# A Macaron block on one core: the experts' first layer as seven block products for four, its operand sums on GpSimd and VectorE, and the slot search of two experts at once

## The chip, the core and the metric

The kernel runs on one core of one Trainium2 chip. The metric is device time in microseconds of one execution. Before the change the median of 9 runs is 836.21 us (830.43 to 840.21). One execution was also taken with the hardware profiler; its own time is 834.38 us.

The engines are named as the profile does: PE is the matrix engine (TensorE), PEld its weight load, DVE the vector engine, ACT the scalar engine, POOL GpSimd, SP the engine that only issues DMAs. L364 is line 364 of the kernel before.

## What is computed

8 x 1024 rows of 256 float32 values go through three residual steps: half a mixture of experts, an attention-like layer with a fast-weight memory, and half the same mixture of experts again. The change concerns the mixture of experts alone:

```python
E, F, CAP = 8, 1024, 320
logits = tokens @ gate_w
probs = softmax(logits)
expert_idx = argmax(probs)
mask1 = one_hot(expert_idx, E)
pos = cumsum(mask1, axis=0) - 1
sec_mask = mask1[:, :, None] * one_hot(pos, CAP)
combine_weights = probs[:, :, None] * sec_mask
expert_input = einsum('tec,td->ecd', sec_mask, tokens)
h = relu(einsum('ecd,edf->ecf', expert_input, w1))
expert_output = einsum('ecf,efd->ecd', h, w2)
out = einsum('tec,ecd->td', combine_weights, expert_output)
```

Each token goes to one expert, and each expert takes its first 320 tokens. `tokens` are layer-normed rows. For each expert `h` is a product of 320 x 256 by 256 x 1024 with a relu (the first layer), and the output is `h` by 1024 x 256 (the second layer). Everything is float32.

## The kernel before

`macaron` (L1276) runs `experts` (the first stage), `attention`, and `experts` again (the second stage). In the profiled execution the first layers of the first stage begin at 53.89 us and those of the second at 661.40 us. The attention between them is not edited. Inside all three the order of the program is the order of the work: `tc.manual_schedule` keeps each engine's instructions as the Python calls emit them, and the waits between engines follow from the tiles that are written and read.

**Finding the slots.** `Slots` (L149) works out which rows each expert gets. `begin(q)` (L197) does the part that two experts share: two matmuls into `d_ps`, an ACT copy into `dg` (L206), a matmul `b_ps` (L209), and a DVE comparison into `began` (L212). `tokens(e)` (L215) then does, for one expert, three matmuls into `r_ps` (L222). They use 64 of PE's 128 rows, the upper or lower half by the expert's parity. Six DVE instructions (L235 to L243; ten for expert 0) make the row numbers `get` and `put` from them. `exps` and `gates` (L174, L178) make the gate values, and `spread` (L187) writes them to DRAM (`gate_d`).

**Rows in and out.** `gather(e)` (L276) fetches an expert's 320 rows by three indirect DMAs that POOL issues (two of 128 rows, one of 64 that is held in a different form), and `gate_of(e)` (L287) its gate values by three more. `center` (L295) subtracts the mean of each row on DVE: `bn_stats`, `bn_aggr` and a subtraction for each of the three row tiles. `turn` (L305) transposes the rows on PE, six transposes into two banks, and two ACT copies (L318) bring them to `xT`, the first layer's moving operand, 2 x 128 partitions by 320 columns. The results go out by indirect DMAs from POOL, one for the 64-row part (L400) and one for each of two tiles of 128 rows (L421).

**Startup of a stage** (L326 to L338). On PE: `begin(0)`, the counts of experts 0 and 1, `begin(1)`, 13 idle matmuls (`keep(13)`, L85, which write to a bank that nobody reads and keep PE running while rows arrive), and the turn of expert 0 with two idle matmuls in it. DVE does tokens 0 and 1, `began` for the next two experts, and centers the rows as they come.

**One expert** (the loop at L351 to L428). POOL first gets the gathers and gates of expert e+2, SP the weights of e+1 (`Weights.load`, L254 and L256, 1 MB each, two buffers), and DVE centers the rows of e+1. Then PE does:
- the first layer, 8 blocks of 128 outputs, each two matmuls of 128x128 weights by 320 columns into one bank (L364), followed by ACT's relu out of the bank (L371);
- the turn of expert e+1;
- the second layer of the 64-row part, 16 matmuls of 128 columns over the two halves of PE's columns (L387), with DVE's scaling and residual into `xh` (L397) and a scatter;
- the second layer of the two full tiles, 8 matmuls of 256 columns each (L411), with DVE (L418) and a scatter after each.

The dictionary `searches` (L340) puts the other searches between the first layer's blocks: the spread and tokens 2 and 3 and `begin(2)` in expert 0, tokens 4 and 5 and `begin(3)` in expert 1, tokens 6 and 7 in expert 2. The PSUM banks are three each with the tags `h` (first layer, `r_ps`, `b_ps`) and `t` (turns, spread), and two with the tag `y` (second layer, idle, `d_ps`).

Of the kernel before, what the change touches and what calls it, by code (L numbers as in the profile page):

```python
# [18 lines left out]
P = 128  # L19
# [3 lines left out]
D = 64  # L23
# [125 lines left out]
class Slots:  # L149
# [10 lines left out]
    def __init__(self, sh, pool, pp, dr, routed):  # L160
        self.sh, self.pool, self.pp, self.dr, self.routed = sh, pool, pp, dr, routed
# [15 lines left out]

    def gates(self):  # L178

        nc, routed = self.sh.nc, self.routed  # L180
        tot = self.pool.tile([P, 2, NI], F32, name="tot")
        nc.vector.tensor_reduce(tot[:, 0], routed.dl.rearrange("p e i -> p i e"), AX.X, ALU.add)
        nc.vector.reciprocal(tot[:, 0], tot[:, 0])
        nc.vector.tensor_tensor(routed.by_tile(tot[:, 1]), tot[:, 0], routed.r16, ALU.mult)
        self.by_row = tot[:, 1]

    def spread(self, _):  # L187

        nc = self.sh.nc
        t_ps = self.pp.tile([P, 512], F32, tag="t", name="t_ps")  # L190
# [6 lines left out]
    def begin(self, q, between=lambda n: None):  # L197

        nc, sh, pool, pp = self.sh.nc, self.sh, self.pool, self.pp

        d_ps = pp.tile([P, 512], F32, tag="y", name="d_ps", bufs=2)
# [6 lines left out]
        b_ps = pp.tile([P, 512], F32, tag="h", name="b_ps")  # L208
# [5 lines left out]

    def tokens(self, e):  # L215

        nc, sh, pool, pp = self.sh.nc, self.sh, self.pool, self.pp
        part = slice(e % 2 * D, (e % 2 + 1) * D)
        r_ps = pp.tile([P, 512], F32, tag="h", name="r_ps")
        rv = r_ps[:, : NS * (P + 1)].rearrange("p (s r) -> p s r", s=NS)  # L220
        for s in range(NS):
            nc.tensor.matmul(  # L222
                rv[:, s, :],
                lhsT=self.began[part, s * P : (s + 1) * P],
                rhs=self.dg[part, e // 2, :],
                start=True,
                stop=True,
            )
# [4 lines left out]
        for a, b in ((0, 1), (1, NS)) if e == 0 else ((0, NS),):  # L233
# [4 lines left out]
            nc.vector.tensor_reduce(t, upto[:, a:b], AX.X, ALU.add)  # L238
            nc.vector.scalar_tensor_tensor(t, t, float(-P), rv[:, a:b, P], ALU.add, ALU.add)
# [6 lines left out]
class Weights:  # L246


    def __init__(self, nc, pool, w1, w2):
        self.nc, self.pool, self.w1, self.w2, self.at = nc, pool, w1, w2, {}  # L250
# [7 lines left out]


def experts(sh, routed, src, dst, weights, dr, name, idle=0):  # L260
# [3 lines left out]

    nc, tc = sh.nc, sh.tc
    with ExitStack() as st:
        rp = st.enter_context(tc.tile_pool(name=f"{name}_r", bufs=1))
        ep = st.enter_context(tc.tile_pool(name=f"{name}_e", bufs=2))
        pp = st.enter_context(tc.tile_pool(name=f"{name}_p", bufs=3, space=PSUM))
# [1077 lines left out]
```

## Time and profile before

| | |
|---|---|
| median of 9 runs | 836.21 us (830.43 to 840.21) |
| the profiled execution | 834.38 us |
| its span, first to last instruction | 832.5 us |
| mean granted PE clock | 0.951 of full speed |
| first layers of stage 1 / stage 2 begin | 53.89 / 661.40 us |
| DVE, ACT, POOL busy | 55%, 42%, 57% of the span |

The page of a profile gives the share of the span for which each engine was busy, then the span in 40 slices (each digit is a busy share in tenths; for the line PEclk it is the clock that PE was granted, 9 is full). The views of the trace used below are the timeline of one engine (start, length, engine, line, operation, output<-inputs, shapes, count, and in brackets how long the engine had been idle and what ended that), the groups (all instructions of one line and shape: busy time and mean duration in ns, then the idle time before them), and windows (busy times of the engines in a stretch). A float32 matmul is two records. "x32" over 8.78 us is thus 16 matmuls. Ends of matmuls are modelled and overlap the next start, so the time that a matmul takes from the engine is read from start to start.

### The profile page before, as it was taken

The numbers are of one execution on the slowest core, as the hardware profiler recorded it, in microseconds if no ns is written. First come the engines' busy times: TensorE is split into PE (matmuls) and PEld (weight loads), VectorE is DVE, ScalarE is ACT, GpSimd is POOL, SyncE is SP. The second block draws the span as 40 slices with busy tenths as digits, with TensorE's granted clock in tenths as the row PEclk, the third lists the DMA queues.
The fourth block names the chain that finished last, engine by engine and source line by source line (L and its number), as shares of the span: only waits on it lengthen the run. The fifth ranks groups of instructions, "written<-read, shape, count | busy, mean of one in ns | idle before, by whom it ended". The sixth has DMA issues, their size and how long they took to land. (4 is left out here: it accounts for less than half of the span.)

```text
span 832.5 us, 13850 instructions
## 1 busy us (share of the span) xinstructions
PE 763.3 (92%) x5304; PEld 554.7 (67%) x5304; DVE 454.5 (55%) x939; ACT 346.6 (42%) x738; POOL 471.3 (57%) x610
## 2 busy tenths in 40 slices
PE   7996899999848999899999999999978988999997
PEld 5665677887625576666757576676764666778875
DVE  7770332222236988888887868978744613322220
ACT  5411212222136585767666755766332212122221
POOL 6525344441123688888888868886754353444411
PEclk9997899999958999999999979999799989999999
DMA  9993345442034233354454523334325623454420
GB/s 299 370 379 115 103 137 184 139 142 67 27 97 103 77 78 103 83 176 100 152 130 135 138 78 110 79 127 103 128 74 179 243 74 93 133 179 139 143 72 19
DMA packets 110946, 110.41 MB, mean 133 GB/s; under 512 B 12384, under 2 KB 103904, under 8 KB 110880
## 3 DMA queue, kind: packets, MB, share of 16 engines
q1 hardware_dynamic: 73312, 66.50, 26.7%
q10 hardware_dynamic: 31680, 31.46, 12.1%
q0 software_dynamic: 5888, 11.57, 4.1%
q8 instruction: 42, 0.69, 0.3%
q14 instruction: 24, 0.20, 0.1%
HBM read 78.80 MB, written 30.64 MB: 131 GB/s over the span
## 5 line engine op out<-in xcount | busy, mean ns | idle before, releaser
L371 ACT ACTIVATE hT<-ph 128x320 f32<-128x320 f32 x128 | 55.6, 437 | 236.1 <-PE ph L364 209.3
L364 PE MATMUL ph<-xT,w1t 128*128 128x320 f32 x512 | 148.0, 442 | 0.9 <-ACT xT L318 0.9
L411 PE MATMUL py<-w2t,hT 128*128 128x256 f32 x512 | 120.4, 394 | 7.2 <-issue 7.2
L364 PEld LDWEIGHTS ph<-xT,w1t 128*128 128x128 f32 x512 | 97.0, 192 | 39.8 <-issue 2.0
L411 PEld LDWEIGHTS py<-w2t,hT 128*128 128x128 f32 x512 | 99.5, 197 | 24.5 <-issue 10.8
L397 DVE SCALAR_TENSOR_TENSOR xh<-py,gate,xg 64x128 f32<-64x128 f32 x32 | 11.2, 350 | 130.8 <-PE py L387 105.9
L418 DVE SCALAR_TENSOR_TENSOR xo<-py,gate,xg 128x256 f32<-128x256 f32 x32 | 15.5, 484 | 95.1 <-PE py L411 91.5
L287 POOL DMA_INDIRECT gate<-gate_d,get x48 | 45.6, 949 | 36.2 <-DMA gate_d<-gates 22.2
L1111 PE MATMUL pre<-wg,xT 128*128 128x256 f32 x256 | 61.7, 402 | 2.6 <-DVE m L870 2.6
L775 PE MATMUL pre<-xT,w 128*64 128x512 f32 x256 | 61.4, 603 | 0.5 <-ACT kk L807 0.5
L1111 PEld LDWEIGHTS pre<-wg,xT 128*128 128x128 f32 x256 | 50.8, 202 | 11.5 <-DVE m L870 3.2
L1155 POOL TENSOR_TENSOR xo<-xo,xr 128x512 f32<-128x512 f32 x32 | 42.9, 1353 | 21.0 <-DVE xo L1149 16.9
L678 ACT ACTIVATE xt<-xt,ln_nm,lx_t 128x256 f32<-128x256 f32 x64 | 34.4, 592 | 24.5 <-POOL ln_nm L673 24.5
L1149 DVE SCALAR_TENSOR_TENSOR xo<-tail,rs,gate 128x256 f32<-128x256 f32 x64 | 27.1, 477 | 25.5 <-DMA out<-xo 15.7
L964 DVE TENSOR_TENSOR gc<-ehd,c 128x1536 f32<-128x1536 f32 x16 | 40.0, 2539 | 0.3
L421 POOL DMA_INDIRECT out<-xo,put x16 | 15.8, 990 | 39.5 <-DVE xo L418 37.3
L421 POOL DMA_INDIRECT x<-xo,put x16 | 15.8, 988 | 39.3 <-DVE xo L418 37.2
L775 PEld LDWEIGHTS pre<-xT,w 128*64 128x64 f32 x256 | 15.8, 136 | 30.4 <-issue 22.4
L876 POOL TENSOR_TENSOR abq<-qq,ab 128x512 f32<-128x512 f32 x16 | 34.5, 2156 | 2.3 <-DMA ab<-kept 2.2
L387 PE MATMUL py<-w2t,hT 128*64 128x128 f32 x512 | 32.7, 276 | 2.5 <-issue 2.5
L400 POOL DMA_INDIRECT out<-xh,put x8 | 8.1, 1008 | 46.9 <-DVE xh L397 46.9
L685 PE MATMUL pre<-ident,xt 128*128 128x128 f32 x128 | 21.0, 298 | 14.7 <-ACT xt L678 13.3
(256 smaller groups left out, 1642.3 us busy)
## 6 DMA issues: line engine op xcount, KB each, us to landing
w1t<-w_in SPq DMA_DIRECT2D x16, 1024.0 KB
w2t<-w_in SPq DMA_DIRECT2D x16, 1024.0 KB
xt<-hidden_in SPq DMA_DIRECT2D x16, 512.0 KB
x<-xt SPq DMA_DIRECT2D x16, 512.0 KB
xt<-x ACTq DMA_DIRECT2D x16, 512.0 KB
xr<-x ACTq DMA_DIRECT2D x16, 512.0 KB
x<-xo ACTq DMA_DIRECT2D x14, 512.0 KB
out<-xo ACTq DMA_DIRECT2D x14, 512.0 KB
```

The source lines that it names most:

```text
L287: nc.gpsimd.indirect_dma_start(out=gate[:, s : s + 1], out_offset=None, in_=slots.gate, in_offset=bass.IndirectOffsetOnAxis(ap=slots.get[: ...
L364: nc.tensor.matmul(ph[:, :CAP], lhsT=a[:, c, f * P : (f + 1) * P], rhs=at[:, c, :], start=(c == 0), stop=(c == 1),)
L371: nc.scalar.activation(hT[:, f, :], ph[:, :CAP], AF.Relu)
L387: nc.tensor.matmul(py[h * D : (h + 1) * D, :P], lhsT=hT[:, f, 2 * P :], rhs=b[:, f, h * P : (h + 1) * P], start=(f == 0), stop=(f == FC - ...
L411: nc.tensor.matmul(py[:, :H], lhsT=hT[:, f, s * P : (s + 1) * P], rhs=b[:, f, :], start=(f == 0), stop=(f == FC - 1),)
L421: nc.gpsimd.indirect_dma_start(out=dst, out_offset=bass.IndirectOffsetOnAxis(ap=slots.put[:, e, s : s + 1], axis=0), in_=xo[:, s, :], in_o ...
L678: self.nc.scalar.activation(x, x, AF.Identity, bias=u.nm[:, j : j + 1], scale=u.r16[:, j : j + 1])
L775: self.nc.tensor.matmul(ps[self.half[r], :], lhsT=self.w3[:, k, f * D : (f + 1) * D], rhs=u.xT[:, k].rearrange("h (p r t) -> h p r t", p=N ...
L876: self.nc.gpsimd.tensor_tensor(u.abq[:, n], u.kv[2], u.ab[:, n], ALU.mult)
L964: self.nc.vector.tensor_tensor(u.gc[:, layer], g.unsqueeze(2).to_broadcast([P, B, 3, D]), u.c3.rearrange("s n j -> s j n").unsqueeze(3).to ...
L1111: self.nc.tensor.matmul(ps[:, q * H : (q + 1) * H], lhsT=u.xT[:, k, j * P : (j + 1) * P], rhs=self.wg[:, k, :], start=(k == 0), stop=(k == 1),
L1155: self.nc.gpsimd.tensor_tensor(u.xo[h][:, two], u.xo[h][:, two], u.xr[h][:, two], ALU.add)
```

## The change

**First layer.** A product of a 2 x 2 block matrix by a 2 x 2 block matrix takes eight block products; with sums of blocks beforehand and afterwards it takes seven (Strassen's method in Winograd's form). Here the blocks of the weights are 128 x 128 (two halves of the 256 inputs, two neighbouring blocks of 128 outputs), and those of the rows are 128 x 160 (the 320 columns in halves, `HC = 160`). For each pair g of output blocks (four pairs for an expert) there are seven matmuls of 160 columns in place of four of 320, so 28 for an expert in place of 16.

The sums of the weights are four `tensor_tensor` of 128 x 512 on GpSimd for each expert, the first two after the first layer of the expert before, the others after its 64-row scatter. They go to a tile `s` of two buffers. The sums of the rows, `row_sums`, are three DVE instructions per expert. The sums of the products are spread over DVE and ACT: each pair of output blocks has an ACT copy (`p6`), four DVE additions (`u`, `v`, one of 320 columns into `hT`, one of 160), and three relus of which two read and write SBUF. The signs are turned so that the centered rows and the relus carry a scale of -1.

```diff
+    def sums(self, e, some):
+        (a11, a12), (a21, a22) = self.parts(e)
+        if e not in self.s:
+            self.s[e] = self.pool.tile([P, 4, FC // 2, P], F32, tag="s", name="s")
+        s = self.s[e]
+        for n in some:
+            x, y, op = (
+                (a21, a22, ALU.add),
+                (s[:, 0], a11, ALU.subtract),
+                (a11, a21, ALU.subtract),
+                (a12, s[:, 1], ALU.subtract),
+            )[n]
+            self.nc.gpsimd.tensor_tensor(s[:, n], x, y, op)
...
+        def row_sums(xT):
+            t = ep.tile([P, 4, HC], F32, tag="xs", name="xs")
+            v = xT.rearrange("p c (j n) -> p (c j) n", j=2)
+            nc.vector.tensor_tensor(t[:, 0:2], v[:, 1:4:2], v[:, 0:2], ALU.subtract)
+            nc.vector.tensor_tensor(t[:, 2], v[:, 3], t[:, 0], ALU.subtract)
+            nc.vector.tensor_tensor(t[:, 3], v[:, 2], t[:, 2], ALU.subtract)
+            return t
...
+            def one(self, g):
+                x = self.x[g] = bank("x", "x")
+                self.product(x[:, :HC], self.s[:, 1], g, self.t[:, 2])
+                self.product(x[:, HC : 2 * HC], self.a[0][0], g, self.b[:, 0, 0], stop=False)
+                u = self.u[g] = ep.tile([P, HC], F32, tag="u", name="u", bufs=3)
+                p6 = ep.tile([P, HC], F32, tag="p6", name="p6")
+                nc.scalar.copy(p6, x[:, :HC])
+                nc.vector.tensor_tensor(u, x[:, HC : 2 * HC], p6, ALU.add)
+            def two(self, g):
+                z = self.z[g] = bank("z", "z")
+                self.product(z[:, :HC], self.s[:, 2], g, self.t[:, 1])
+                self.product(z[:, HC : 2 * HC], self.a[1][1], g, self.t[:, 3])
+                self.product(z[:, 2 * HC : 3 * HC], self.s[:, 0], g, self.t[:, 0], stop=False)
+                v = ep.tile([P, 1, HC], F32, tag="v", name="v")
+                nc.vector.tensor_tensor(v[:, 0], z[:, :HC], self.u[g], ALU.add)
+                nc.vector.tensor_tensor(
+                    self.hT[:, 2 * g + 1, :].rearrange("p (j n) -> p j n", j=2),
+                    z[:, HC : 3 * HC].rearrange("p (j n) -> p j n", j=2),
+                    v.to_broadcast([P, 2, HC]),
+                    ALU.add,
+                )
+            def three(self, g):
+                x = self.x[g]
+                self.product(x[:, HC : 2 * HC], self.a[0][1], g, self.b[:, 1, 0], start=False)
+                nc.scalar.activation(self.hT[:, 2 * g, :HC], x[:, HC : 2 * HC], AF.Relu, scale=-1.0)
+            def four(self, g):
+                z = self.z[g]
+                self.product(z[:, 2 * HC : 3 * HC], self.s[:, 3], g, self.b[:, 1, 1], start=False)
+                nc.vector.tensor_tensor(self.hT[:, 2 * g, HC:], z[:, 2 * HC : 3 * HC], self.u[g], ALU.add)
+            def relu(self, f, a=0):
+                h = self.hT[:, f, a:]
+                nc.scalar.activation(h, h, AF.Relu, scale=-1.0)
...
+            for g in range(G):
+                first.one(g)
+                if g > 0:
+                    first.three(g - 1)
+                first.two(g)
+                if g > 0:
+                    first.four(g - 1)
+                    first.relu(2 * g - 1)
+                    first.relu(2 * g - 2, HC)
             if e + 1 < E:
-                xT = turn(xn)
+                xT = ep.tile([P, 2, CAP], F32, tag="xT", name="xT")
+                turn(xn[e + 1], 0, xT)
+            first.three(G - 1)
+            first.relu(2 * G - 1)
+            if e + 1 < E:
+                turn(xn[e + 1], 1, xT)
+            first.four(G - 1)
+            first.relu(2 * G - 2, HC)
+            if e + 1 < E:
+                weights.sums(e + 1, (0, 1))
+                t = row_sums(xT)
```

The PSUM banks are now two each for `t`, `x`, `z` and `y`. The 64-row part takes its blocks in the order 0 to 5, 7, 6. `center` keeps `bn_stats` and `bn_aggr` on DVE and has ACT form mean minus row; it works on expert e+2 and stands after the first full tile of the second layer. The gates of an expert are fetched one expert ahead, not two.

**Searches.** `tokens` is split. `counts(q)` does the matmuls of two experts in turns, one on each half of PE's rows, into two banks; `in_two(e)` does an expert's DVE part from them.

```diff
+        for s in range(NS):
+            for r in range(2):
+                part = slice(r * D, (r + 1) * D)
+                nc.tensor.matmul(
+                    self.count[r][:, s, :],
+                    lhsT=self.began[part, s * P : (s + 1) * P],
+                    rhs=self.dg[part, q, :],
+                    start=True,
+                    stop=True,
+                )
```

The searches that remain in the loop stand after the 64-row part (`search(e, 0)` and `search(e, 1)`): `begin(2)` in expert 0, the counts and tokens of 4 and 5 in expert 1, `begin(3)` in expert 2, the counts and tokens of 6 and 7 in expert 3. Those of experts 2 and 3 move to the startup:

```diff
         keep(idle)
-        slots.begin(0, keep)
-        rows, gates = [], []
+        slots.begin(0, "y", keep)
+        slots.exps()
+        slots.counts(0)
+        rows, gates, xn = [], [], {}
         for e in range(2):
             slots.tokens(e)
             rows.append(gather(e))
-        slots.begin(1)
-        slots.exps()
+        weights.sums(0, range(4))
+        slots.begin(1, "y")
+        slots.totals()
+        slots.counts(1)
+        slots.tokens(2)
         keep(13)
-        xT = turn(center(rows[0]), keep)
+        third = slots.in_two(3)
+        xn[0] = center(rows[0], (0,))
         slots.gates()
+        center(rows[0], (1,), xn[0])
+        next(third)
+        center(rows[0], (2,), xn[0])
+        next(third, None)
+        rows.append(gather(2))
+        xT = ep.tile([P, 2, CAP], F32, tag="xT", name="xT")
+        for c in range(2):
+            turn(xn[0], c, xT, keep)
+        t = row_sums(xT)
+        slots.spread()
+        xn[1] = center(rows[1])
+        gates = [gate_of(0), gate_of(1)]
```

In the startup the turn of expert 0 is two turns of three transposes, each with two idle matmuls in it, so four in all.

## The prediction

> **What bounds the kernel now.** I read the page's busy shares and its 40 slices first. In them PE's weight-load line is called PEld.
>
> ```profile
> PE 763.3 (92%) x5304; PEld 554.7 (67%) x5304; DVE 454.5 (55%) x939; ACT 346.6 (42%) x738; POOL 471.3 (57%) x610
> ...
> PE   7996899999848999899999999999978988999997
> ...
> PEclk9997899999958999999999979999799989999999
> ```
>
> PE is busy for 92% of the span, and every other engine for under 60%. So a stage costs what PE takes for it, plus the waits that reach PE. The attention between the two expert stages is not edited, and I leave its time as it is. The clock line has dips (the 7 and the 5, the two 7s later); those in the expert stages come back below.
>
> Then PE's timeline, where a row is start, length, engine, line, and in brackets the idle time before it. Expert 6 of the second stage is an undisturbed expert:
>
> ```profile
> 790.64 8.78 PE L364 MATMUL ph<-xT,w1t 128*128 128x320 f32 x32
> 799.25 0.86 PE L312 MATMUL pt<-ident,xn 128*128 128x128 f32 x6
> 800.04 1.97 PE L387 MATMUL py<-w2t,hT 128*64 128x128 f32 x32
> 801.94 7.17 PE L411 MATMUL py<-w2t,hT 128*128 128x256 f32 x32
> ```
>
> No brackets: PE never waits. The next expert's L364 starts at 808.95. From start to start the expert takes 18.31 us: first layer 8.61, turn 0.79, 64-row part 1.90, two token tiles 7.01. A float32 matmul is two records, so 16 matmuls are 32 records and one record of 320 columns is 8.61 / 32 = 269 ns. In the second layer one of 256 columns is 7.01 / 32 = 219 ns, of 128 columns (the turns and the two-half pairs aside) about 109.
>
> The windows by expert show that the first experts of a stage are not like that (columns: length; busy time of PE, PEld, DVE, ACT, POOL; granted clock; DMA):
>
> ```profile
> 53.89:85.59 31.70, 24.62 (x121) 18.58 (x122) 8.42 (x27) 4.95 (x13) 13.42 (x14) 0.84 0.54 178
> 85.59:111.92 26.33, 23.07 (x121) 17.48 (x120) 8.56 (x27) 4.30 (x11) 8.73 (x9) 0.94 0.39 122
> ```
>
> Expert 0 of the first stage takes 31.7 us. Expert 2 takes 20.44. The searches of expert 0 account for 3.2 (two trains of 0.86, one `begin` of 1.2, a spread of 0.27); 31.7 - 18.31 - 3.2 = 10.2 are lost. By the same sum the lost time is 5.1 and 0.4 in experts 1 and 2, and 7.2, 3.9 and 0.4 in the second stage (28.72, 25.13 and 20.44 us there): 27 us in all. The largest piece, on PE and on DVE:
>
> ```profile
> 79.27 6.49 PE L411 MATMUL py<-w2t,hT 128*128 128x256 f32 x16 [6.73 <-issue]
> ```
> ```profile
> 78.50 0.71 DVE L397 SCALAR_TENSOR_TENSOR xh<-py,gate,xg 64x128 f32<-64x128 f32 x2 [14.01 <-remote]
> ```
>
> PE stands 6.73 us for nothing that the profile shows, and then runs the second tile in 6.32 us instead of 3.50, at half clock. I can't say what releases it, and this is the main doubt of the sum.
>
> **Part 1, the first layer.** Before: 16 matmuls of 320 columns, 8.61 us. After: per pair of blocks 7 products of 160 columns, 28 per expert. The trace has no 160-column matmul. Between 109 ns (128 columns) and 219 (256) a line gives 0.86 ns a column, so 136 ns a record, 0.272 a product, 28 x 0.272 = 7.62: **-0.99 us** an expert, if PE never waits.
>
> It will wait. The sums after the products are a chain: `two(g)` needs the z bank that `four(g-2)`'s DVE addition left, and the loop has two z banks. From that addition's end to the next one of the same parity: PE hears it (0.055, the latency seen between DVE and PE) and runs up to the third product (about 1.02 with its drain), DVE does v (0.32) and hT (0.49), PE's `four` lies under these, DVE adds (0.32): 2.16 us for each g with the gaps. PE's own work for a g is 7 x 0.272 = 1.90. The stall is 0.26 at g = 2 and 3, **+0.52**. The DVE durations are estimates between rows of the trace with one PSUM operand: 128 wide 0.29, 256 wide 0.42, 384 wide 0.55. At 0.40 and 0.60 nothing is gained, at 0.30 and 0.47 there is 0.6. I take -0.47 for the 14 experts with a successor (the split turn covers the loop's tail) and +0.1 for the two last: **-6.4 us**, bounds 0 and -13.9.
>
> **Part 2, the searches.** Before, six trains of 0.87 us stand in each stage's stream (L222, six records each). After, the counts of two experts go over alternate halves of the rows. The startup shows the price, because two trains are adjacent there:
>
> ```profile
> 647.81 1.26 PE L222 MATMUL r_ps<-dg,began 64*128 64x129 f32 x12
> 649.00 0.49 PE L203 MATMUL d_ps<-tri,mask_b 128*128 128x128 f32 x2
> ```
>
> 12 records in 1.19 us. Two such pairs remain in the stream (the third moves to the startup): 5.2 - 2.4 = 2.8 a stage, **-5.6 us**. At no gain from alternating it is 1.7 a stage; no less.
>
> **Part 3, the startup.** In before the 13 idle matmuls ran while DVE worked through the first searches:
>
> ```profile
> 650.07 0.38 PE L209 MATMUL b_ps<-dg,before 128*128 128x1 f32 x2 [0.36 <-ACT dg L206]
> 650.31 8.63 PE L85 MATMUL idle<-jrow,ident 128*128 128x384 f32 x26
> 658.78 0.38 PE L312 MATMUL pt<-ident,xn 128*128 128x128 f32 x2
> ...
> 661.40 0.81 PE L364 MATMUL ph<-xT,w1t 128*128 128x320 f32 x2 [0.45 <-ACT xT L318]
> ```
>
> After, `counts(1)` stands ahead of them in PE's order and needs `began(1)`, which DVE ends at 46.02 (653.87 in the second stage). So: 46.05 + 1.3 of counts = 47.35; 8.46 of idle matmuls = 55.8; two turns in sequence with four idle matmuls, 0.80 + 4 x 0.65 + 0.45 of copy = 3.85; row_sums 0.47 + 0.31 + gaps = 0.9; first product at 60.6, against 53.89. That is +6.7, and by the same sum +7.0 in the second stage: **+13.7 us**. What DVE does here besides (token 2, the split centre) ends under the idle matmuls; it is worth up to 3 us a stage if it doesn't.
>
> **Part 4, GpSimd.** Four 128x512 additions per expert join POOL's queue. Before, an expert has nine indirect DMAs at 1.25 to 1.29 us from start to start:
>
> ```profile
> 717.51 0.99 POOL L276 DMA_INDIRECT xg<-x,get  x1 [0.30 <-issue]
> 718.80 0.97 POOL L276 DMA_INDIRECT xg<-x,get  x1 [0.30 <-issue]
> ```
>
> That is 7.6 for gathers and gates and 3.8 for scatters, the third of which waits about 1.3 more for the landing of the second. Now the rows for the additions:
>
> ```profile
> L1155 POOL TENSOR_TENSOR xo<-xo,xr 128x512 f32<-128x512 f32 x32 | 42.9, 1353 | 21.0 <-DVE xo L1149 16.9
> L876 POOL TENSOR_TENSOR abq<-qq,ab 128x512 f32<-128x512 f32 x16 | 34.5, 2156 | 2.3 <-DMA ab<-kept 2.2
> ```
> ```profile
> L985 POOL TENSOR_TENSOR go<-st,last 128x512 f32<-128x512 f32 x7 | 17.1, 2436 | 0.5
> ```
>
> At 1.35 each the queue's cycle is 7.6 + 5.4 + 3.8 + 1.3 = 18.1 us, against PE's 18.31 - 0.47 = 17.8 with no search: level. The second half of the sums has about 2.6 us of slack to the next expert's `two(0)`, and only experts 1 to 5 have all nine transfers, so I cost it at nothing. Its cover ends at about 1.65 us a sum. Bounds: nothing, and +4.7 an expert at 2.43.
>
> One rule bears on that price. The Trainium skill ("SBUF — State Buffer", section "SBUF: two separate sides") says that a DVE operation with two SBUF inputs and a GpSimd operation that reads SBUF exclude each other for the whole instruction. L876's mean of 2.16 beside L1155's 1.35 agrees: single L876 rows of 3.28 lie beside a DVE scan of 3.08. By the rule the three row_sums (both inputs SBUF) may stand behind a sum of the first half, or the sum behind them, up to 1.4 us an expert on PE's path, 20 us in all. I don't count it: PE has 8.9 us of second layer between row_sums and the next first layer.
>
> **The sum**, against the profiled execution's own 834.38 us (span 832.5; the median of the runs is 836.21, so 1.8 are added): -6.4 - 5.6 + 13.7 = +1.7. What decides is whether the late start is paid in full. The first stall of each stage lies 19 us (first stage) and 15 us (second) behind the first product. If what ends it is an event fixed in time and not a result of PE, then a start that is 7 us later runs into less of it: 6.7 of the first, and of the second's 7.2 lost us about 5.5, come back. -12.2 + 1.7 = -10.5: 823.9, as a median **826 us**.
>
> **The rivals.** (A median within 0.5%, some 4.2 us, can't be told from no change here.)
> - **Covered start**, the forecast, 826. For it: no engine's work explains the 6.73 us. Against: a stall that follows PE would move along. 0.42.
> - **Start paid in full**: +1.7, so 838 (836 to 841). For it: everything in part 3 is a plain chain. 0.25.
> - **The lost time shrinks**: the lost 27 us lie only where searches stand within the first layer; these leave it. With three quarters of 27 gone and the start paid: 834.4 + 1.7 - 20, 816; 812 with cover. 0.17.
> - **GpSimd becomes the bound**, on the other side: place, the queue gathers - sums - scatters of experts 1 to 5; point, 1.65 us a sum. At 1.72 it costs about 4 a stage (834 with the covered start, 846 without); at L985's 2.43, 4.7 x 5 x 2 less the slack, 40: 866. Sums that read 128-element runs have no row here. 0.16.
>
> Range 812 to 846. Faster: 0.41 of the first and all of the third, 0.58. Within 0.5%: most of the second and a little of the fourth, 0.18. Slower: 0.24.
>
> **What would show it.** First product near 60.6 and 668.4 (else part 3 is wrong). An undisturbed expert (6 of the second stage) of about 17.8 us, with brackets of about 0.26 at the z products; none, and it is 17.3; above 18.3, and DVE's chain is longer than I take. Counts of two experts in 1.2 to 1.3. Sums of 1.3 to 1.4 on POOL, and PE rows of the first product that wait for `s`, if the fourth rival holds. A long idle PE within expert 0 that ends near 79 us, if the cover is real; near 86, if it moves along; none, and the third rival holds. The forecast is wrong if that stall moves, or if POOL is late for the sums.

## The result: slower by 4.0%

The changed kernel's median is 870.03 us (10 runs, 864.01 to 881.68), the kernel before 836.05 (31 runs). The ratio is 1.040, with a 95% interval of 1.036 to 1.043. The profiled execution has a span of 874.4 us against 832.5. The forecast said 826, with a range of 812 to 846.

The page of the changed kernel, the lines that were read first in the kernel before:

```profile
PE 773.4 (88%) x5696; PEld 590.4 (68%) x5696; DVE 552.0 (63%) x1195; ACT 387.5 (44%) x914; POOL 553.3 (63%) x674
...
PE   7977889998938999899999999999787898888897
...
PEclk9989999999968999998899999999988998989999
```

PE is busy for 10 us more, not for less, and the span is 42 us longer. Its line falls to 8 and once 7 over the expert stages at the left and the right, where it had 9 for most experts. DVE has 98 us more work.

Where the 41.9 us lie, from the starts of the first layers in PE's timelines of the two kernels:

| part | before | after | difference |
|---|---|---|---|
| first product of stage 1 | 53.89 | 64.26 | +10.4 |
| experts 0 to 6, stage 1 | 151.7 | 158.4 | +6.7 |
| expert 7, both stages | 34.8 | 35.5 | +0.7 |
| attention | | | -0.3 |
| `begin(0)` to first product, stage 2 | 15.7 | 25.8 | +10.1 |
| experts 0 to 6, stage 2 | 147.6 | 161.9 | +14.4 |

Half of the loss is in the two startups, half in the experts. By expert, stage 2 went from 28.7, 25.1, 20.4, 18.3, 18.3, 18.3, 18.3 us to 24.3, 25.8, 22.3, 25.5, 21.4, 23.5, 19.2. Expert 0 did become shorter; experts 3 to 5, which never waited before, now take 3 to 7 us more each (of which 0.9 in expert 3 is a search that was moved there).

**The startup**, PE's timeline of the changed kernel:

```profile
47.05 1.66 PE L230 MATMUL r_ps<-dg,began 64*128 64x129 f32 x12 [3.45 <-DVE began L216]
48.64 10.54 PE L85 MATMUL idle<-jrow,ident 128*128 128x384 f32 x26
...
64.26 0.51 PE L392 MATMUL x<-xs,s 128*128 128x160 f32 x2 [1.26 <-DVE xs L372]
```

The counts of experts 2 and 3 wait for DVE, as forecast. What the forecast didn't count is what that wait does: the counts then take 1.6 us from start to start where they take 0.87 at full clock, and the 13 idle matmuls 10.4 us instead of 8.5, because the clock has dropped while PE stood: the granted clock in the windows of these two stretches is 0.50 and 0.82, and in the kernel before it is 1.00 all the way from 36 us to the first product.

**An expert**, expert 1 of stage 2. First DVE, then PE, then POOL:

```profile
720.69 0.32 DVE L404 TENSOR_TENSOR u<-x,p 128x160 f32<-128x160 f32 x1 [1.27 <-ACT p L403]
724.64 0.33 DVE L413 TENSOR_TENSOR v<-z,u 128x160 f32<-128x160 f32 x1 [3.62 <-remote]
```
```profile
720.12 0.43 PE L392 MATMUL z<-xs,s 128*128 128x160 f32 x2
...
725.54 0.90 PE L392 MATMUL z<-xT,s 128*128 128x160 f32 x2 [3.40 <-DVE hT L414]
```
```profile
722.13 0.95 POOL L335 DMA_INDIRECT gate<-gate_d,get  x1 [0.30 <-issue]
723.10 1.27 POOL L295 TENSOR_TENSOR s<-w1t 128x512 f32<-128x512 f32 x1
```

`v` needs `u` (there at 721.01) and the three z products (the last one's record ends at 720.6). It starts at 724.64. The trace has PE's semaphore counts too: none arrives between 721.71 and 724.62, and then five arrive within 0.19 us, which stand for products and transposes that take PE over 1 us to do. So PE had done them; **its signals came late**. PE then waits for DVE's `hT`, and the loop through the first layer carries each late signal on. In the changed kernel such runs of late signals are in most experts. Each ends 1.0 to 1.8 us, mostly 1.5, after the row of the last of the three gate transfers (here that row is 722.13 to 723.08, and the signals come at 724.62).

The 6.73 us "issue" and the 14.01 us "remote" of the kernel before look like the same thing, in experts 0 and 1 only. PE finished the 64-row part by 68.9 there, DVE's `xh` began at 78.50 and ended at 79.21, which gives back the bank that the second tile writes, and PE went on at 79.27. So PE stood for DVE, and DVE for a signal of PE: PE's semaphore counts have none between 67.01 and 78.48. Twelve indirect transfers run beside it, and here the signals come while the last one is being issued (78.11 to 79.05). Single gate values, or any run of such transfers: that is the lead that the experiments followed.

### The profile page after: what moved, and what is told of

It reads as the page before. It is cut to its first block, busy times and chain, and to the rows that moved or that the text cites. A ratio compares the mean times of both kernels' runs of the same rounds, so it can differ in the third digit from the quotient of the medians.

```text
span 874.4 us, 15310 instructions
## 1 busy us (share of the span) xinstructions
PE 773.4 (88%) x5696; PEld 590.4 (68%) x5696; DVE 552.0 (63%) x1195; ACT 387.5 (44%) x914; POOL 553.3 (63%) x674
## 3 DMA queue, kind: packets, MB, share of 16 engines
q1 hardware_dynamic: 73312, 66.50, 25.5%
## 5 line engine op out<-in xcount | busy, mean ns | idle before, releaser
L545 PEld LDWEIGHTS py<-w2t,hT 128*128 128x128 f32 x512 | 97.0, 192 | 19.2 <-DVE xh L528 4.5
L435 ACT ACTIVATE hT<-hT 128x320 f32<-128x320 f32 (+1 forms) x128 | 51.5, 404 | 75.9 <-DVE hT L431 58.8
L351 ACT ACTIVATE xn<-xg,ln 128x256 f32<-128x256 f32 x48 | 24.4, 508 | 117.5 <-DVE ln L350 114.8
L392 PE MATMUL z<-xs,s 128*128 128x160 f32 x256 | 59.5, 314 | 7.3 <-DVE hT L431 4.5
L392 PE MATMUL x<-xT,w1t 128*128 128x160 f32 x256 | 50.6, 308 | 4.4 <-DVE u L404 3.5
L392 PEld LDWEIGHTS z<-xs,s 128*128 128x128 f32 x256 | 41.1, 191 | 15.0 <-DVE hT L431 12.1
L413 DVE TENSOR_TENSOR v<-z,u 128x160 f32<-128x160 f32 x64 | 20.8, 325 | 37.8 <-remote 17.4
L392 PE MATMUL z<-xT,s 128*128 128x160 f32 x128 | 30.9, 324 | 15.3 <-DVE hT L414 13.8
L517 PE MATMUL py<-w2t,hT 128*64 128x128 f32 x512 | 41.1, 320 | 3.3 <-ACT hT L435 3.0
L392 PEld LDWEIGHTS x<-xT,w1t 128*128 128x128 f32 x256 | 39.0, 191 | 6.6 <-DVE u L404 4.7
L404 DVE TENSOR_TENSOR u<-x,p 128x160 f32<-128x160 f32 x64 | 20.8, 324 | 32.8 <-ACT p L403 25.9
L295 POOL TENSOR_TENSOR s<-w1t 128x512 f32<-128x512 f32 x32 | 41.0, 1280 | 0.7
```

What stands on the lines that cost most here:

```text
L295: self.nc.gpsimd.tensor_tensor(s[:, n], x, y, op)
L351: nc.scalar.activation(xn[:, s, :], xg[:, s, :], AF.Identity, bias=ln[:, 6:7], scale=-1.0)
L392: nc.tensor.matmul(out, lhsT=a[:, g, :], rhs=b, start=start, stop=stop, skip_group_check=True)
L435: nc.scalar.activation(h, h, AF.Relu, scale=-1.0)
L517: nc.tensor.matmul(py[h * D : (h + 1) * D, :P], lhsT=hT[:, f, 2 * P :], rhs=b[:, f, h * P : (h + 1) * P], start=(f == order[0]), stop=(f = ...
L545: nc.tensor.matmul(py[:, :H], lhsT=hT[:, f, s * P : (s + 1) * P], rhs=b[:, f, :], start=(f == 0), stop=(f == FC - 1),)
```

## The experiments

The runs lay on five chips, and the kernel before took between 812 and 837 us on them. So each run is compared with the kernel before on its own chip.

**First theory:** the transfers of single gate values hold PE's signals to the other engines. **Rivals:** the sums on GpSimd (late, or in DVE's way), or DVE's chain of sums alone.

### Four kernels on one chip (the kernel before: 813.6 us)

`a_gates_late`: the gates of e+1 behind the 64-row scatter.

```diff
-                gates.append(gate_of(e + 1))
                 weights.load(e + 1)
...
                 bounds_check=2 * NT - 1,
                 oob_is_err=False,
             )
+            if e + 1 < E:
+                gates.append(gate_of(e + 1))
             if e + 1 < E:
                 weights.sums(e + 1, (2, 3))
```

> The changed kernel with one move: the gate values of expert e+1 are fetched after the 64-row scatter of expert e and not ahead of the first layer of e (expert 0 keeps its own three transfers in its first layer; expert 1's no longer stand there). Theory of the gate transfers: while the three transfers of single 4-byte gate values run, PE's signals to the other engines come late, and are let go about 1.5 us after the last one is issued; in the first layer DVE and PE wait for each other at each step, so each expert loses 2 to 7 us. With the transfers gone from there an expert is near 18.5 us plus its search: about 25 us less in each stage, 815 to 835 in all. Rival, the sums on GpSimd (signals are let go 0.2 us after the first sum ends): the sums still come after three gathers, only 3.8 us sooner; the stalls stay, 860 to 872. Rival, the chain of sums on DVE: no difference, 866 to 874.

842.1 us, ratio 1.036 (1.026 to 1.046).

`a_gates_out`:

```diff
-                gates.append(gate_of(e + 1))
+                gates.append(gate1)
```

`gate1` is a constant tile, for experts 0 and 1 too.

> The changed kernel without gate transfers: all gate values are a constant tile, so the output is not the reference's (each expert's output is scaled by 0.5). Theory of the gate transfers: no stall left in the first layers; 810 to 830, and under a_gates_late by the three transfers that expert 0 kept (2 to 8 us). Rival, the sums on GpSimd or the chain on DVE: 860 to 874.

836.1 us, ratio 1.024 (1.016 to 1.033).

`a_rows_for_gates`, against a_gates_late:

```diff
+                more_rows(e + 1)
                 weights.load(e + 1)
```

> As a_gates_late, but in the place where the gate transfers stood, three transfers of whole rows (128 x 1 KB, into a tile that nobody reads; the rows' tile has three buffers in place of four). POOL's queue is as long as in the changed kernel. If only the transfers of 4-byte values hold PE's signals: within 5 us of a_gates_late. If any run of six indirect transfers does, or the length of POOL's queue: within 6 us of the changed kernel's 870.

875.3 us, ratio 1.074 (1.066 to 1.082).

`b_gates_late`, the kernel before:

```diff
                 rows.append(gather(e + 2))
-                gates.append(gate_of(e + 2))
...
                 oob_is_err=False,
             )
+            if e + 1 < E:
+                gates.append(gate_of(e + 1))
```

> The kernel before with the same move of the gate transfers, the first layer and the searches as they were. Theory of the gate transfers: the unexplained 27 us of experts 0 to 2 (there the transfers lie beside searches, turns and the 64-row part, whose matmul records are 107 to 109 ns) shrink by 12 to 22 us: 814 to 824. Otherwise 832 to 838.

813.9 us, ratio 1.000 (0.996 to 1.003).

The chip answered another question: it has no late signals, not even in the kernel before, which is 22 us faster here, so nothing was there to be removed. What the four do show is the queue on GpSimd. In a_gates_late the gate transfers stand ahead of the second half of the sums, and PE waits 10.1 us for sums. a_rows_for_gates was built wrongly: I wrote that its queue is as long as the changed kernel's, but it has the gates and the rows, three transfers more; there PE waits 28.3 us for sums. The tipping point of the forecast's fourth rival is real, and near. In the changed kernel itself, PE's waits name no sum among the largest (2.2 us in all in a_again, which comes next).

### The changed kernel without late signals, and its startup and queue (the kernel before: 812.2 us)

`a_again`, the changed kernel as it is:

> The changed kernel as it is, beside the kernel before on this chip. In the four runs so far the kernel before took 813.6 us in place of 836, and PE's signals were never late in any trace. If late signals are a matter of the chip (or of its state) and not of the gate transfers: where they are absent, about 836 against 813 (+20 us of startups, the experts near even), without bunched signals in the trace; where they are present, about 870 against 836. If the gate transfers cause them everywhere: over 860 against 813.

841.4 us, ratio 1.037 (1.031 to 1.043). So the changed kernel loses nearly the same share where signals are in time, and late signals can't be the whole cause. First product 62.12; an expert with nothing in its way takes 18.55 us; but experts 2, 4 and 6 of stage 1 take 24.1, 21.6 and 20.2.

`a_startup`:

```diff
         slots.totals()
+        keep(5)
         slots.counts(1)
-        slots.tokens(2)
-        keep(13)
-        third = slots.in_two(3)
+        keep(7)
+        second, third = slots.in_two(2), slots.in_two(3)
...
-        for c in range(2):
-            turn(xn[0], c, xT, keep)
+        pts = [bank("z", "pt") for _ in range(2)]
+        for s in range(NS):
...
+            if s == 1:
+                keep(1)
         t = row_sums(xT)
+        next(third)
+        next(third, None)
```

> The changed kernel with another order in the startup: five idle matmuls ahead of the counts of experts 2 and 3 and seven behind (not thirteen behind), the turn of expert 0 by row tiles with both halves at once and one idle matmul (not two turns with four), and DVE's tokens of expert 3 after row_sums. If the startup's loss is PE's order (counts, then idle matmuls, then two turns): the first product near 57 us in place of 64.3, so 6 to 8 us less in each stage, 12 to 16 in all. Rival, the rows or the sums on GpSimd set the first product: under 4 us in all.

836.3 us, ratio 1.030 (1.024 to 1.036), some 5 us under a_again; 12 to 16 were expected. The first product of stage 1 comes at 56.30, 5.8 us sooner, but expert 0 takes 24.2 us and not 21.0. DVE and ACT still have the tokens of expert 3 and the centring of expert 1 ahead of the first `u`, so PE waits 2.7 us there: half the gain went into the next wait.

`a_order`, against a_gates_late:

```diff
             if e + 1 < E:
-                weights.sums(e + 1, (0, 1))
                 t = row_sums(xT)
...
-            if e + 1 < E:
-                weights.sums(e + 1, (2, 3))
...
+            if e + 1 < E:
+                weights.sums(e + 1, range(4))
             first, hT = First(e, xT, t), None
```

> The changed kernel with POOL's queue in another order: gathers of expert e+2, all four sums of e+1, the 64-row scatter, the gates of e+1, the two other scatters. The work is the same. If GpSimd's queue is nearly as long as an expert, as in the forecast, but not longer: within 4 us of a_again where PE's signals are in time. If gate transfers beside the first layer hold the signals: 20 us or more under a_again where they are late. If a longer queue binds: PE's waits for sums appear and it is over a_again.

830.4 us, ratio 1.025 (1.019 to 1.031), 11 us under a_again; within 4 was expected. The lead is in a_again's DVE timeline, at the end of expert 1, with POOL's beside it:

```profile
93.50 2.29 DVE L371 TENSOR_TENSOR xs<-xT 128x320 f32<-128x320 f32 x1 [0.30 <-ACT xT L364]
95.83 1.28 DVE L372 TENSOR_TENSOR xs<-xT,xs 128x160 f32<-128x160 f32 x1
...
99.30 0.16 DVE L257 SCALAR_TENSOR_TENSOR tok<-tok,r_ps 128x3 f32<-128x3 f32 x1
99.49 2.44 DVE L258 TENSOR_SCALAR get<-tok 128x3 int32<-128x3 f32 x1
...
103.61 0.17 DVE L258 TENSOR_SCALAR get<-tok 128x3 int32<-128x3 f32 x1
```
```profile
94.16 1.27 POOL L295 TENSOR_TENSOR s<-w1t 128x512 f32<-128x512 f32 x1
95.51 1.41 POOL L295 TENSOR_TENSOR s<-s,w1t 128x512 f32<-128x512 f32 x1
...
99.41 1.28 POOL L295 TENSOR_TENSOR s<-w1t 128x512 f32<-128x512 f32 x1
100.63 1.27 POOL L295 TENSOR_TENSOR s<-w1t,s 128x512 f32<-128x512 f32 x1
```

Row_sums (L371 to L373) take 3.9 us here beside the first two sums and 1.1 apart from them. An operation on three numbers per row takes 2.44 us when it meets the other two, until the second one ends, and 0.17 us otherwise. DVE then has no pause until 106.6 and is behind with the tokens, the residual and the centring; the next expert's `u` comes late, and PE stands 2.71 us in the first layer of expert 2. In a_order the mean of `get` falls from 0.98 to 0.33 us, and PE's waits for `u` from 10.4 to 2.7 us.

It takes both delays, as two more runs tell. In a_gates_out, on the other chip with signals in time, the first two sums end ahead of row_sums and only `get` stands:

```profile
95.32 0.49 DVE L371 TENSOR_TENSOR xs<-xT 128x320 f32<-128x320 f32 x1 [0.30 <-ACT xT L364]
95.84 0.32 DVE L372 TENSOR_TENSOR xs<-xT,xs 128x160 f32<-128x160 f32 x1
...
98.82 2.34 DVE L258 TENSOR_SCALAR get<-tok 128x3 int32<-128x3 f32 x1
```

There expert 2 takes 20.2 us and not 24.1, and PE's waits for `u` are 1.9 us in all. In a_order it is row_sums that stand (41.1 us in all, against 33.3 in a_again) and `get` that is nearly free. So the forecast named the right meeting, costed it at 1.4 us an expert and then at nothing, because PE has 8.9 us of second layer in between. What it left out is the rest of DVE's work in these 8.9 us, and the second delay: `get` has one SBUF operand, and the rule that the forecast cited is about two.

`a_all`: a_startup's and a_order's edits, and three z banks.

```diff
-        bank = lambda tag, name: pp.tile([P, 512], F32, tag=tag, name=name)
+        bank = lambda tag, name: pp.tile(
+            [P, 512], F32, tag="y" if tag == "t" else tag, name=name, bufs=2 if tag == "x" else 3
+        )
```

> Both of these, and three banks for the three products in place of two (the turn's banks are shared with the second layer's, three in all). If the wait for a bank (0.25 us at each of two groups, and about 0.1 for each restart) is what made the seven products slower than the sixteen: first layer and turn 9.64 us become 8.9 to 9.1, so 0.6 an expert, 8 us in all, on top of the startup's 12 to 16: 20 to 26 us under a_again. If DVE's chain binds and not the bank: 14 to 17 under.

820.0 us, ratio 1.008 (1.004 to 1.012), 21 us under a_again. An undisturbed expert is 17.87 us and not 18.55. The third group of one first layer, in a kernel with two z banks (a_gates_out2, which comes below) and then in a_all, on PE's timeline:

```profile
777.35 0.71 PE L392 MATMUL x<-xT,w1t 128*128 128x160 f32 x4
778.14 0.54 PE L392 MATMUL z<-xs,s 128*128 128x160 f32 x2
778.52 0.43 PE L392 MATMUL z<-xs,w1t 128*128 128x160 f32 x2
```
```profile
775.83 0.71 PE L394 MATMUL x<-xT,w1t 128*128 128x160 f32 x4
776.37 0.43 PE L394 MATMUL z<-xs,s 128*128 128x160 f32 x2
776.64 0.43 PE L394 MATMUL z<-xs,w1t 128*128 128x160 f32 x2
```

With two banks the z product starts 0.79 us after the x products, with three 0.54 (four records of 0.136): 0.25 us is the wait for the bank. Then the next product comes after 0.38 us and not 0.27: a product that had to wait costs 0.1 us more, and the view gives no name to that. First layer and turn are 9.64 us with two banks, 8.96 with three.

### What is left when the products go (the kernel before: 829.6 us)

`a_plain`: the searches, the startup and the centring of the change, without sums, and in the place of the products:

```diff
+            for f in range(FC):
+                ph = bank("x" if f % 2 else "z", "ph")
+                for c in range(2):
+                    nc.tensor.matmul(
+                        ph[:, :CAP],
+                        lhsT=w1t[:, c, f * P : (f + 1) * P],
+                        rhs=xT[:, c, :],
...
+                nc.scalar.activation(hT[:, f, :], ph[:, :CAP], AF.Relu, scale=-1.0)
```

> The changed kernel with the first layer of the kernel before (16 matmuls of 320 columns and eight relus an expert; no sums on GpSimd, DVE or of products), and the rest of the change kept: searches of two experts at once and behind the 64-row part, startup, centring on ACT, gates one expert ahead. If the seven products with their sums are what costs: an expert of 18.31 us plus its search (1.2 or 0.9), no lost time in experts 0 to 3, so about 132.5 us for the first seven experts against 137.9 before, and what is left over the kernel before is the startup's 7 us a stage: ratio 0.997 to 1.008. If the searches or the centring on ACT cost (DVE is late for the next first layer): experts 2 and 4 stay over 20 us, ratio over 1.015.

824.2 us, ratio 0.994 (0.990 to 0.998): 0.6% under the kernel before, with the late startup still in it (first product 62.56). Its trace has no wait put down to "remote", while the kernel before has them on this chip (b_again below) and is 17 us slower than on the chip of a_again. So part of this gain is the kernel before's loss. Its first seven experts take 134.8 us in stage 1 and 134.6 in stage 2. An expert without a search is 18.61 us (the split turn takes 1.08 and not 0.79), so the searches cost 4.4 us a stage, where the kernel before needed 9.8 even without late signals (137.9 in b_gates_late, less 7 x 18.31).

`a_sums_first`, against a_order:

```diff
             if 0 < e < E - 1:
                 weights.load(e + 1)
+            if e + 1 < E:
+                weights.sums(e + 1, range(4))
+            if 0 < e < E - 2:
+                rows.append(gather(e + 2))
...
-            if e + 1 < E:
-                weights.sums(e + 1, range(4))
             first, hT = First(e, xT, t), None
```

> The changed kernel with all four sums of expert e+1 at the head of POOL's queue of expert e, then the gathers, the 64-row scatter, the gates, the other scatters: as a_order, but the sums lie beside the first layer, where DVE only works out of PSUM, and not beside row_sums and the search's small DVE operations. If a sum on GpSimd shuts DVE's operations from SBUF to SBUF out (row_sums of 1.3 to 1.9 us and a token operation of 2.4 us were seen beside sums, 0.33 and 0.17 apart from them): these rows go back to 0.2 to 0.5 us; 9 to 14 us under the changed kernel (841 on such a chip). If not: row_sums stay over 1 us, and the time is that of a_order or more.

842.2 us, ratio 1.016 (1.011 to 1.021). `get` 0.29 us, row_sums 0.56, 0.44 and 0.38 us. The rows nearly go back to their lengths. The chip is not a_again's, so the 9 to 14 us can only be read between ratios (1.037 there), and even these flatter: the kernel before takes 829.6 us here and 812.2 there.

`a_best`: a_all with that order, and in the startup

```diff
         for e in range(2):
             slots.tokens(e)
-            rows.append(gather(e))
-        weights.sums(0, range(4))
+            if e == 0:
+                rows.append(gather(e))
+                weights.sums(0, range(4))
+        rows.append(gather(1))
```

> a_all with the sums at the head of POOL's queue as in a_sums_first, and in the startup the sums of expert 0 ahead of the gather of expert 1, with the small token operations of expert 2 behind the centring. If the shut-out of DVE by the sums was what a_all still lost (a first product at 58.9, experts 1 and 3 of the second stage at 23 us): first product near 55.5, no expert over 20.5 but the first; 797 to 806, ratio 0.98 to 0.993. If it was not: 812 to 820, ratio over 1.0.

833.3 us, ratio 1.001 (0.997 to 1.006): a miss. The first product is at 55.08 as expected, but expert 0 takes 27.4 us (PE waits 4.9 us there for `u`, which stands behind the centring of expert 1 in DVE's queue; the rows for it are now fetched behind four sums) and expert 6 22.9. There PE waits 0.8 us for `u`, behind the centring, whose rows landed late, and 2.0 us for a relu that waits for "remote": no semaphore count of PE arrives from 182.70 to 185.54, beside the gate transfers. With the sums at the head of POOL's queue the gathers come 5 us later, and the centring waits for them; but this chip also has late signals, and one run doesn't tell the two apart.

`b_again`, the kernel before as it is, on the same chip:

> The kernel before, for its trace on this chip. If late signals of PE belong to a chip: none of the waits of experts 0 to 2 that the forecast could not explain, experts 0, 1 and 2 at 22.5, 21.7 and 20.4 us, and 812 in place of 836.

826.6 us, one run. The trace has late signals in experts 0 and 1 of stage 1 (33.3 and 27.7 us) and fewer in stage 2 (26.0 and 22.2). So chips differ in degree: this one lies between the others.

### On a chip with late signals (the kernel before: 837.0 us)

`a_again2`, the changed kernel as it is:

> The changed kernel as it is once more, to stand beside the two next ones on this chip. If late signals appear: 855 to 875, with waits of 2 to 7 us in the first layers; if they do not: 837 to 845.

873.7 us, ratio 1.045 (1.038 to 1.053). DVE's waits of this run hold the line

```profile
DVE v L413 <- remote: 21.8, 6, 4.2
```

(total, times, longest), and 6.9 us more of the same before `hT`.

`a_gates_out2`, the edit of a_gates_out:

> The changed kernel without gate transfers (a constant gate: the output is not the reference's). If PE's signals are late on this chip and gate transfers are what holds them: no such waits, first seven experts 136 us a stage, 20 to 30 us under a_again2. If another thing holds them: as a_again2, less up to 10. If no signals are late on this chip: 0 to 8 us under a_again2, and nothing is told apart.

836.3 us, ratio 0.999 (0.996 to 1.003), 37 us under a_again2. No wait of DVE or ACT is put down to "remote". The first seven experts take 136.6 and 137.1 us and not 164.4 and 157.0. Not all 37 are late signals: where signals are in time, leaving the gate transfers out also saved some 5 us (a_gates_out 836.1, a_again 841.4, on two chips). Without these transfers the kernel takes 836 us on either kind of chip.

`a_rows_only`, against a_gates_out2 (and the same for experts 0 and 1 ahead of the loop):

```diff
                 gates.append(gate1)
+                more_rows(e + 1)
```

> As a_gates_out2, with three transfers of whole rows (1 KB each, into a tile that nobody reads; the rows' tile has three buffers) where the three gate transfers stood, so that POOL's queue has the changed kernel's length (a_rows_for_gates had three transfers more than it). If 4-byte values hold the signals: as a_gates_out2. If any run of six indirect transfers does: as a_again2. If the chip has no late signals: as a_again2, within 5 us, since only POOL's queue is left.

860.3 us, ratio 1.029 (1.022 to 1.037), between the two. "Remote" waits of DVE and ACT are 14.2 us, against 29.5 in a_again2 and none in a_gates_out2. So on a chip that shows late signals **the run of indirect transfers holds them**; three transfers of 4-byte values in it hold them about twice as long as three of whole rows, by one trace each. The first theory is right in its place and too narrow in its cause. Why the signals wait, and why only on some chips, stays open: no view shows it.

`a_plain_best`: a_plain with a_startup's order.

> a_plain with the startup's order of a_startup (idle matmuls around the counts of experts 2 and 3, one turn by row tiles). a_plain's first product came at 62.6 us against 54.3 before; without the sums of expert 0 nothing shuts DVE out here. If the startup's loss adds to the rest as it stands: first product near 54.5, 7 to 8 us less in each stage than a_plain, so a ratio to before of 0.973 to 0.985. If an earlier start is lost again in expert 0 (as it was in a_startup, where expert 0 took 24.2 us in place of 21.0): 0.985 to 0.994.

819.2 us, ratio 0.980 (0.976 to 0.985). It keeps the gate transfers where the change put them and has 8.2 us of "remote" waits on DVE and ACT, against 29.5 in a_again2. With records of 269 ns, PE has about half as many signals and matmuls beside these transfers as with 136 ns, and DVE stands outside its loop. That this is the reason is argued, not shown.

### The better version once more (the kernel before: 812.2 us)

`a_plain_best2`, the kernel of a_plain_best:

> a_plain_best again, beside it on this chip: a ratio to before of 0.975 to 0.99 (0.980 on the chip of its first run).

808.2 us, ratio 0.996 (0.993 to 0.999).

`a_plain_late`, a_plain_best with the gate transfers moved as in a_gates_late:

> a_plain_best with the gate transfers of expert e+1 behind the 64-row scatter of expert e, beside the second layer's full tiles, where PE signals another engine only at the end of a tile. If the late signals of a_plain_best (8 us in its trace, 10 us in experts 1 and 2 of the first stage) come from the run of six transfers: none left, experts 1 and 2 at 19.5 and 19.9 us in both stages; 0 to 10 us under a_plain_best2, ratio to before 0.965 to 0.982. If the place of the gates makes no difference: within 3 us of a_plain_best2.

810.6 us, ratio 0.998 (0.995 to 1.002), within 3 us of a_plain_best2. This chip has no late signals, so whether moving the gates is enough is open. a_plain_best is the version that beats both kernels: by 2% where signals come late and 0.4% where they don't. A stretch of its PE timeline, from a_plain_best2, shows an expert without a wait:

```profile
745.60 8.78 PE L443 MATMUL ph<-xT,w1t 128*128 128x320 f32 x32
754.22 1.16 PE L359 MATMUL pt<-ident,xn 128*128 128x128 f32 x6
```

## Why the prediction was wrong, step by step

- **"The sum", the covered start (-12.2): failed, and it decided the sign of the forecast.** Expert 0 did get shorter, by 4.9 and 4.4 us. But the sum took the stall for something with a fixed end in time. It comes with runs of indirect transfers, and the change puts the gate transfers beside the first layer of every expert up to 6 and makes the first layer dense in signals. Late signals cost the kernel before some 25 us (837.0 against 812.2 on two chips) and the changed kernel some 32 (873.7 against 841.4): some 7 more where 12 less was forecast. They don't make the sign of the measured change, which is 29 us where no signal is late. That "no engine's work explains the 6.73 us" was a misreading: `xh` at 78.50, a line that the prediction shows, gives back the bank.
- **Part 3, the startup (+13.7): right in mechanism, too small.** The startups cost +10.4 and +10.1 us in place of 6.7 and 7.0. In stage 1 the missing 3.7 are the counts and idle matmuls at a lowered clock after the 3.45 us wait (0.3 and 1.9), the turns and row_sums (0.5), and the stage itself, which began 1.0 us later.
- **Part 1, the first layer (-6.4): wrong sign.** The durations were right (u 0.324, v 0.325, hT 0.492, last addition 0.317 us; products 0.272), and so was the stall at the bank, 0.25 (0.26 was forecast, though the terms listed for it add up to 0.3). First layer and turn take 9.64 us where 8.9 was forecast and 9.40 was before. The first 26 products take 7.77, which is 0.2 over products and stalls: 0.1 for each restart. The last two products and the split turn take 1.87 where 1.33 was taken: the split turn doesn't cover the loop's tail, and that is the larger miss. With a third bank it is 8.96.
- **Part 2, the searches (-5.6): too small.** Two experts' counts take 0.87 us, not 1.19. a_plain's searches cost 4.4 us a stage, 5.4 less than before, so -11 in all, where the products are gone.
- **Part 4, GpSimd at nothing: failed.** A sum took 1.27 to 1.28 us, under the forecast's 1.35, and PE's waits for sums are small (2.2 us in a_again). But the sums held up row_sums and `get` on DVE, and DVE then kept PE waiting for `u`. On a chip without late signals, another order of POOL's queue (a_order) is worth 11 us. Two figures of this part don't follow from its rows: 4 x (2.43 - 1.35) is 4.3 and not 4.7, and the 1.65 us that the cover is said to bear isn't derived.
- **The rivals.** The one that ended on the slower side (GpSimd, up to 866) had nearly the right time for the wrong reason: the queue was not the bound. "The lost time shrinks" holds in part in a_plain_best, where the products are gone: on the chip with late signals its first seven experts lose some 10 us to them, against 24 in the kernel before.

What the parts are worth together, on chips without late signals: a_again is 29 us over the kernel before. The startups hold 18 of it (7.8, and 10.5 between the end of stage 1 and the first product of stage 2); the experts, 144.3 and 140.7 us against 137.9 and 137.4, hold the rest. In a_order the experts take 136.2 and 137.1 us, as many as before, and the startups are what is left.

## What to carry to other kernels

Count what fewer multiplications bring in what they wait for: seven products for eight save 0.99 us of PE an expert at best and bought a chain through DVE that had to answer within each 1.9 us, so every disturbance of DVE became PE's. A wait that no row explains isn't a cushion; until its cause is known, bound it from both sides, as a thing that the change may also multiply. And when two engines share something, look for the price at every operation that lies beside the other's, not only at the one that was added, and add the delays up along the queue in which they stand.

## What the runs showed of the hardware

- DVE's `tensor_scalar` and `tensor_tensor` from SBUF to SBUF stood until a GpSimd `tensor_tensor` ended: 0.17 became 2.44 us (`get`), 0.33 became 1.27 (row_sums). `began`, which reads one number a row from PSUM and the rest from SBUF, took 1.44 to 1.47 us beside sums and 0.42 to 0.58 apart from them. Reductions and `bn_stats` beside the same sums kept their 0.55 and 0.42 us, and DVE operations with a whole operand in PSUM kept theirs. Of the two cases that the Trainium skill names ("SBUF — State Buffer", section "SBUF: two separate sides": a DVE operation in a 2-port mode, or one with two SBUF inputs), `get` is not the second, since it has one SBUF input; no run here tells whether it is the first.
- PE's signals to the other engines can come late while a run of indirect transfers from GpSimd is under way (waits put down to "remote" of up to 4.4 us in the changed kernel, 14.0 in the kernel before), and then arrive 0.04 to 0.05 us apart. Some chips show it, others don't: the kernel before took 837 and 812 us there.
- The wait of 3.45 us in the startup made the next 13 idle matmuls 10.4 us long where they had been 8.5, at a granted clock of 0.82 and 1.00.
